# A convolution chain in fp32: group 0's first layer from raw row copies, and M products on quarters of ij

## The chip, the cores and the metric

The kernel runs on one core of one Trainium2 chip. The metric is the device time of one execution in microseconds, the median of several runs. The engines named below are TensorE (PE in the profile; its weight loads are PEld), VectorE (DVE), ScalarE (ACT), GpSimd (POOL) and SyncE (SP, which here only issues loads).

## The reference, cut to what matters

The input `x` is 4 x 32 x 32 x 16 (batch, row, column, channel). Three convolution layers and one interval layer are added to it, each on a group-normalized copy:

```python
def conv_ref(inputs, M, W, G):                 # layers 0, 1 and 3
    first = einsum('ijyx,byxc->bijc', M, inputs)          # the "M product"
    shifted = conv3x3(inputs, kernels from G)             # 32*32*16 filters of 3x3x16
    diff = relu(inputs - shifted)                         # (layer 3 the same, in another layout)
    second = einsum('ijyx,bijyxc->bijc', W, diff)
    return first - second

def _gn(v, G=8, eps=1e-5):                     # mean and variance over (h, w, 2 channels), per batch
    ...
x = x + conv_ref(_gn(x), L0...)
x = x + conv_ref(_gn(x), L1...)
x = x + interval_ref(_gn(x), L2...)            # pooling over intervals, small matmuls, sigmoids
x = x + conv_ref(_gn(x), L3...)
```

Every one of the 1024 positions (i, j) has its own 3x3 filter per feature. The convolution is computed as matmuls of filters with a matrix of shifted rows of the image (`im`), and the subtraction of `inputs` is folded into the filters (`pick`).

## The kernel before

The batches form two groups of two (`NG = 2`, `GB = 2`), so `GC = 32` columns of (batch, channel) per group. Layers and groups alternate in six phases. A phase runs over eight chunks of 128 positions (i, j), 16 features and 2 batches: 256 steps of six matmuls (in three slots) and one eviction.

```python
# one step (f, b) of conv_layer
ps = bank_pair(...)                            # 3 of these in PSUM
for slot in range(3):
    for h in range(2):                         # two halves of the image, on rows 0-63 and 64-127 of the array
        r = slice(64 * h, 64 * h + 64)
        w, v = (W9[r], im9v[r, b]) if slot == 2 else (W[r, slot], imv[r, slot, b])
        nc.tensor.matmul(ps[:, h, :], lhsT=w[:, f % FU, :], rhs=v[:, :, :H],
                         start=slot == 0, stop=slot == 2)
nc.vector.scalar_tensor_tensor(junk, ps, 0.0, chunks[n], op0=ALU.min, op1=ALU.mult,
                               accum_out=acc[...])
wait -= 1
if wait <= 0:
    wait = next(behind, 1 << 20)               # work of the next phase, spread between the steps
```

Eight features of filters come in one load (`raw`, four buffers). `prep` subtracts `pick` on GpSimd and scales slot 2 on ScalarE into `W9`; `prep_rest` (the halving step) finishes `W9` on VectorE. `W9` and `im9` are in fp32r, and carry the ninth tap.

Before a convolution the group is normalized, turned, written to DRAM and gathered back as shifted rows:

```python
def before_conv(g, layer, on_pe=False):
    xn = work.tile([P, NT, GC], F32, tag="xn", bufs=2)
    yield from group_norm(g, ..., xn, on_pe)   # sums, mean, xc, squares, rstd, xn
    nc.vector.transpose(xt[g][:, :, 1 : 1 + H], xn)
    for r in range(ROWS):
        (nc.scalar if r % 2 else nc.sync).dma_start(inner[:, r], xt[g][GC * r : GC * (r + 1)])   # xs <- xt
    for slot, row, tap in ...:                 # 12 of them, for 2 halves: 24 loads
        (nc.scalar, nc.sync)[at % 2].dma_start(
            im[g][r0 : r0 + C, slot, :, :RUN], xsv[:, :, off : off + RUN])                         # im <- xs
    halve(im9[g], im[g][:, 2], low_x)          # ScalarE
    halve_rest(im9[g], im[g][:, 2], low_x)     # VectorE
```

For five of the six phases this runs beside the phase ahead. For the first phase it stands alone at the start:

```python
nc.scalar.dma_start(X[0], x[0])
load_raw(0); load_chunk(0)                     # on SyncE's queue
...
start = before_conv(*phases[0], on_pe=True)    # sums across partitions by a matmul with ones
next(start)
# ... pick, low_w, low_x from the identity ...
for _ in start: pass
prep(0); prep_rest(0)
for phase in range(len(phases)):
    conv_layer(phase, behind(phase))
```

The M product of a layer and group, once per phase, in the stream of `behind`:

```python
def first_term(g, layer):
    fs = work.tile([P, 2, 512], F32, tag="fs")
    for half in range(2):                      # halves of ij
        mt = wpool.tile([P, NT, 512], F32, tag="MT", bufs=1)
        nc.sync.dma_start(mt, convs[layer][0][half])
        yield 12
        ps = bank(...)                         # pf
        for pt in range(NT):                   # eight parts of the sum over (y, x), on four column groups
            j = pt % 4
            nc.tensor.matmul(ps[32 * j : 32 * j + 32, :], lhsT=xn[:, pt, :], rhs=mt[:, pt, :],
                             start=pt < 4, stop=pt >= 4, tile_position=(0, 32 * j))
        nc.scalar.copy(fs[:, half, :], ps)
        yield 2
    ps = bank(...)                             # pfs
    for t in range(NT):                        # add the four partial sums and turn
        nc.tensor.matmul(ps[:, GC * t : GC * (t + 1)],
                         lhsT=fs[:, t // 4, t % 4 * P : (t % 4 + 1) * P], rhs=stack, start=True, stop=True)
    yield 2
    nc.vector.tensor_tensor(X[g], X[g], ps..., ALU.add)
```

The four column groups of the array (32 columns each, by `tile_position`) each hold a partial sum over a quarter of the terms; the matmuls with `stack` (four identities of 32 on top of each other) add them.

Of the kernel before, what the change touches and what calls it, by code (L numbers as in the profile page):

```python
# [14 lines left out]
P = 128  # L15
B, H, C = 4, 32, 16
NG = 2
# [20 lines left out]
def net_kernel(ctx: ExitStack, tc: tile.TileContext, x, convs, iv_w, iv_b, out):  # L38
# [30 lines left out]
    nc.scalar.dma_start(X[0], x[0])  # L69
# [16 lines left out]
    load_raw(0)  # L86
    load_chunk(0)


    ones = const.tile([P, P], F32, name="ones")  # L90
    nc.vector.memset(ones, 1.0)
# [29 lines left out]
    im = [const.tile([P, 3, GB, PITCH], F32, name=f"im{g}") for g in range(NG)]  # L121
    im9 = [const.tile([P, GB, PITCH], F32R, name=f"im9{g}") for g in range(NG)]

    def zeros(g):

        nc.gpsimd.memset(xt[g], 0.0)
        nc.gpsimd.memset(im[g][:, 2], 0.0)
        for y in (0, HP - 1):
            nc.gpsimd.dma_start(xs[g][:, y * HP : (y + 1) * HP], zero[:GC])

    nc.gpsimd.memset(zero, 0.0)
    zeros(0)

    def prep(u):

        if u >= n_chunks * NU:
            return
        raw = raws.pop(u)
        f0 = u % NU * FU
        nc.gpsimd.tensor_tensor(  # L140
            raw[:, 1], raw[:, 1],
            pick[:, f0 : f0 + FU].unsqueeze(2).to_broadcast([P, FU, P]),
            ALU.subtract,
        )
        W9 = wpool.tile([P, FU, P], F32R, tag="W9", name=f"W9_{u}")
        halve(W9, raw[:, 2], low_w)
        units[u] = (raw, W9)

    def prep_rest(u):
        if u in units:  # L150
            raw, W9 = units[u]
            halve_rest(W9, raw[:, 2], low_w)
# [9 lines left out]
    def group_norm(g, name, dst, on_pe=False):  # L162
# [9 lines left out]
        def mean_of(part, name):  # L172
            if not on_pe:
                m = work.tile([P, GC // 2], F32, tag="sum", name=f"sum_{name}")
                nc.gpsimd.partition_all_reduce(m, part, channels=P, reduce_op=bass_isa.ReduceOp.add)  # L175
                return m
            ps = bank(f"ps_{name}")
            nc.tensor.matmul(ps[:, : GC // 2], lhsT=ones, rhs=part, start=True, stop=True)  # L178
            return ps[:, : GC // 2]
# [25 lines left out]
    def before_conv(g, layer, on_pe=False):  # L205
        xn = work.tile([P, NT, GC], F32, tag="xn", bufs=2, name=f"xn_{g}_{layer}")
        xns[g] = xn
        yield from group_norm(g, f"c{g}{layer}", xn, on_pe)
# [27 lines left out]
    def first_term(g, layer):  # L236
# [3 lines left out]
        fs = work.tile([P, 2, 512], F32, tag="fs", name=f"fs_{g}{layer}")  # L240
        for half in range(2):
            mt = wpool.tile([P, NT, 512], F32, tag="MT", bufs=1, name=f"MT_{g}{layer}{half}")
            nc.sync.dma_start(mt, convs[layer][0][half])
            yield 12
            ps = bank(f"pf_{g}{layer}{half}")
# [339 lines left out]
```

## Time and profile before

| | |
|---|---|
| time, median of 3 runs | 3106.62 us (3105.61 to 3107.74) |
| span of the profiled execution | 3100.8 us |
| convolution matmuls, fp32 slots | 12288 entries of 64x512, mean 589 ns, overlapping |
| evictions (junk) | 1536, mean 1224 ns |
| M products (pf) | 192 entries, mean 598 ns; busy 23.1 us |
| adding the partial sums (pfs) | 96 entries, six blocks |
| HBM traffic | 211.64 MB read, 69 GB/s over the span |

The page gives the busy time of each engine, its course over 40 slices of the span, the chain of work that ended last (followed back from the last instruction), and the costliest groups of instructions by line, with output and inputs by their names in the program. In a row of the timeline the columns are start, length, engine, line, operation, tiles and shape, and in brackets the idle time of the engine just before and what ended it. An fp32 matmul shows as two entries. Names such as pc, pf and pfs are the PSUM tiles of the convolution, of the M product and of its summation; ps_l is a small matmul of the interval layer; xs and xt are the DRAM and SBUF forms of the turned input.

### The profile page before, as it was taken

Reading aid. Unit: us, or ns where it says so; the run is one execution under the profiler, and the core shown is the slowest. Engines: PE = TensorE matmul, PEld = TensorE weight load, DVE = VectorE, ACT = ScalarE, POOL = GpSimd, SP = SyncE. Lnnn points to the kernel's source line nnn. Section 1 sums busy time; section 2 is a strip of 40 time slices with the busy share of each in tenths; the row PEclk is TensorE's granted clock in tenths of the full one; section 3 lists DMA queues with packets and bytes.
Section 4 is the critical chain, followed back from the end, with each engine's and each line's share of the span. In section 5 each row is a group of like instructions: output and inputs, shape, how many; then the busy total and the mean of one; then the engine's idle time right before and its main releaser. Section 6 shows DMA issues by size and latency. Waiting matters only on the chain.

```text
span 3100.8 us, 37902 instructions
## 1 busy us (share of the span) xinstructions
PE 3069.8 (99%) x15760; PEld 1506.1 (49%) x15760; DVE 2114.4 (68%) x3361; ACT 145.7 (5%) x151; POOL 294.3 (9%) x182
## 2 busy tenths in 40 slices
PE   6999999999999999999999999999999999999999
PEld 3444444444444544444445444444544444454544
DVE  5666666766666666666678876668876666666666
ACT  0000000000000000000000000000000000000000
POOL 1100000100000000000012310001330000000000
PEclk9999999999999999999999999999999999999999
DMA  4331111421111141211111113121113211121100
GB/s 143 125 129 49 51 66 48 125 75 68 48 64 60 53 141 48 75 48 68 48 58 65 48 69 126 48 75 48 68 48 110 91 48 70 48 75 48 68 28 2
DMA packets 37068, 215.19 MB, mean 69 GB/s; under 512 B 11808, under 2 KB 12320, under 8 KB 23072
## 3 DMA queue, kind: packets, MB, share of 16 engines
q1 hardware_dynamic: 29472, 207.02, 18.6%
q10 hardware_dynamic: 7296, 5.74, 0.9%
q8 instruction: 123, 2.02, 0.3%
q14 instruction: 49, 0.40, 0.0%
q0 software_dynamic: 128, 0.02, 0.0%
HBM read 211.64 MB, written 1.12 MB: 69 GB/s over the span
## 4 chain that ended last, share of the span: by engine, by line
PE 99%; DMA 1%; DVE 0%; issue 0%; ACTq 0%; ACT 0%; DVEq 0%
PE pc L463 97%; PE pf L248 1%; PE pfs L256 0%; DMA im<-xs 0%; DMA X<-in_x 0%; DVE junk L473 0%; PE ps_r L376 0%; PE ps_l L365 0%; DMA xs<-xt 0%; PE ps_l L363 0%; DVE xc_c L188 0%; DVE pp L323 0%; PE ps_y L427 0%; PE ps_vc L178 0%; DVE xt L212 0%
## 5 line engine op out<-in xcount | busy, mean ns | idle before, releaser
L463 PE MATMUL pc<-im,raw 64*128 64x512 f32 x12288 | 2907.4, 589 | 15.3 <-DMA im<-xs 13.3
L473 DVE SCALAR_TENSOR_TENSOR junk<-pc,WT 128x1024 f32<-128x1024 f32 x1536 | 1879.7, 1224 | 958.5 <-PE pc L463 953.2
L463 PEld LDWEIGHTS pc<-im,raw 64*128 64x128 f32 x12288 | 1187.5, 186 | 1185.1 <-issue 800.5
L463 PE MATMUL pc<-im,W 64*128 64x512 f32 x3072 | 1251.1, 804 | 0.0
L463 PEld LDWEIGHTS pc<-im,W 64*128 64x128 f32 x3072 | 298.7, 186 | 365.8 <-issue 364.8
L140 POOL TENSOR_TENSOR raw<-raw,pick 128x1024 f32<-128x1024 f32 x96 | 182.5, 1902 | 1989.2 <-DMA raw<-in_g 1835.6
L111 ACT ACTIVATE W<-raw,low_w 128x1024 fp32r<-128x1024 f32 x96 | 110.4, 1150 | 2268.9 <-PE pc L463 2233.0
L114 DVE SCALAR_TENSOR_TENSOR W<-raw,low_w,W 128x1024 fp32r<-128x1024 f32 x96 | 134.6, 1402 | 0.0
L473 DVE DVE_READ_ACCUMULATOR junk<-pc,WT 128x1 f32 x1536 | 127.2, 83 | 0.0
L396 POOL TENSOR_TENSOR dp_a<-ft_a,rt_r 128x1089 f32<-128x1089 f32 x16 | 39.0, 2445 | 76.3 <-DVE s_a L403 49.5
L396 POOL TENSOR_TENSOR dp_b<-ft_b,rt_r 128x1089 f32<-128x1089 f32 x16 | 37.1, 2325 | 94.6 <-ACT ft_b L389 47.8
L248 PE MATMUL pf<-MT,xn 128*32 128x512 f32 x192 | 23.1, 598 | 0.0
L403 DVE TENSOR_REDUCE s_b<-dp_b 128x33 f32<-128x1089 f32 x16 | 20.5, 1282 | 0.0
L403 DVE TENSOR_REDUCE s_a<-dp_a 128x33 f32<-128x1089 f32 x16 | 20.5, 1282 | 0.0
L175 POOL PARTITION_ALL_REDUCE sum_mc<-part_mc x5 | 2.2, 445 | 188.3 <-DVE part_mc L167 188.3
L252 ACT COPY fs<-pf 128x512 f32<-128x512 f32 x12 | 7.0, 585 | 240.7 <-PE pf L248 240.7
L114 DVE SCALAR_TENSOR_TENSOR im<-im,low_x,im 128x1088 fp32r<-128x1088 f32 x6 | 8.1, 1347 | 13.3 <-DMA im<-xs 13.3
L485 DVE TENSOR_TENSOR X<-X,acc 128x32 f32<-128x32 f32 x48 | 11.8, 246 | 1.5
L256 PEld LDWEIGHTS pfs<-stack,fs 128*128 128x128 f32 x96 | 11.2, 191 | 3.4 <-issue 3.4
L338 DVE TENSOR_TENSOR pp<-pp 64x1024 f32<-64x1024 f32 x10 | 12.1, 1213 | 0.0
L343 DVE TENSOR_TENSOR pp<-pp 64x1024 f32<-64x1024 f32 x10 | 12.1, 1212 | 0.0
L175 POOL PARTITION_ALL_REDUCE sum_mi<-part_mi x2 | 0.9, 446 | 116.2 <-DVE part_mi L167 116.2
(77 smaller groups left out, 136.9 us busy)
## 6 DMA issues: line engine op xcount, KB each, us to landing
raw<-in_g SPq DMA_DIRECT2D x96, 1536.0 KB, 6.7
WT<-in_w SPq DMA_DIRECT2D x48, 512.0 KB, 6.5
MT<-in_mt SPq DMA_DIRECT2D x12, 2048.0 KB, 8.1
im<-xs SPq DMA_DIRECT2D x72, 67.8 KB, 3.0
im<-xs ACTq DMA_DIRECT2D x72, 67.8 KB, 3.0
xs<-xt SPq DMA_DIRECT2D x12, 34.0 KB, 2.8
xs<-xt ACTq DMA_DIRECT2D x12, 34.0 KB, 3.0
X<-in_x ACTq DMA_DIRECT2D x2, 128.0 KB, 7.3
```

The costliest lines, as they stand in the source:

```text
L111: nc.scalar.activation(dst, src, AF.Copy, scale=mask[:, 1:2])
L114: nc.vector.scalar_tensor_tensor(dst, src, mask[:, 0:1], dst.bitcast(F32), op0=ALU.mult, op1=ALU.add)
L140: nc.gpsimd.tensor_tensor(raw[:, 1], raw[:, 1], pick[:, f0 : f0 + FU].unsqueeze(2).to_broadcast([P, FU, P]), ALU.subtract,)
L248: nc.tensor.matmul(ps[32 * j : 32 * j + 32, :], lhsT=xn[:, pt, :], rhs=mt[:, pt, :], start=pt < 4, stop=pt >= 4, tile_position=(0, 32 * j),)
L256: nc.tensor.matmul(ps[:, GC * t : GC * (t + 1)], lhsT=fs[:, t // 4, t % 4 * P : (t % 4 + 1) * P], rhs=stack, start=True, stop=True,)
L338: nc.vector.tensor_tensor(pp[k][:, :H, M:], a[:, :H, M:], a[:, s : H + s, M:], ALU.max)
L343: nc.vector.tensor_tensor(pp[k][:, :H, M:], a[:, :H, M:], a[:, :H, M - s : M - s + H], ALU.max)
L396: nc.gpsimd.tensor_tensor(t, ft[:, i, :].unsqueeze(1).to_broadcast([P, T1, T1]), rt, ALU.add,)
L403: nc.vector.tensor_reduce(s[:, i - 1, :], last, axis=AX.X, op=ALU.max)
L463: nc.tensor.matmul(ps[:, h, :], lhsT=w[:, f % FU, :], rhs=v[:, :, :H], start=slot == 0, stop=slot == 2,)
L473: nc.vector.scalar_tensor_tensor(junk, ps.rearrange("p h n -> p (h n)"), 0.0, chunks[n], op0=ALU.min, op1=ALU.mult, accum_out=acc[:, t, co ...
L485: nc.vector.tensor_tensor(X[g][:, t], X[g][:, t], acc[:, t], ALU.add)
```

## The change

It has two parts.

**The start.** For the first phase (group 0, layer 0) the host gives the shifted rows of the raw input, `xi`, in the very layout of `im`, with zeros at the border, and a copy `xq` of the group's input with (quarter of the image, batch, channel) on the 128 partitions. The kernel loads both, takes mean and variance from `xq` with three small matmuls against masks, and normalizes `im` in place: subtract the mean, multiply by the reciprocal of the standard deviation, and set what lies outside the image to zero again. It works on batch 0 first, the filters of the first load are split in two parts (two features, then six), and the first 16 steps of the first chunk are sorted so that batch 0's eight features come before batch 1's. Batch 1 is normalized on GpSimd beside these steps, and the usual group norm of group 0, which the M product still needs, moves into the stream beside the convolution. What this is for: to start the convolution without the way through DRAM.

**The M product.** Each column group of the array now takes a quarter of ij instead of a part of the sum: all eight parts are added in PSUM, so no summation of partial sums is needed. VectorE turns the result by 32x32 blocks straight from PSUM, for which the host orders M's columns.

```diff
-    nc.scalar.dma_start(X[0], x[0])
+    XQ = const.tile([P, 256], F32, name="XQ")
+    nc.sync.dma_start(XQ, xq)
...
-    load_raw(0)
+    F0 = 2
+    raws[0] = wpool.tile([P, 3, FU, P], F32, tag="raw", bufs=4, name="raw_0")
+    nc.sync.dma_start(im[0][:, :, 0], xi[0])
+    nc.scalar.dma_start(raws[0][:, :, :F0], convs[0][2][0, 0][:, :, :F0])
     load_chunk(0)
+    nc.sync.dma_start(raws[0][:, :, F0:], convs[0][2][0, 0][:, :, F0:])
+    nc.sync.dma_start(im[0][:, :, 1], xi[1])
...
     def first_term(g, layer):
         xn = xns[g]
-        fs = work.tile([P, 2, 512], F32, tag="fs", name=f"fs_{g}{layer}")
+        ps = bank(f"pf_{g}{layer}")
         for half in range(2):
-            mt = wpool.tile([P, NT, 512], F32, tag="MT", bufs=1, name=f"MT_{g}{layer}{half}")
+            mt = wpool.tile([P, NT // 2, 4, 256], F32, tag="MT", bufs=1, name=f"MT_{g}{layer}{half}")
             nc.sync.dma_start(mt, convs[layer][0][half])
             yield 12
-            ps = bank(f"pf_{g}{layer}{half}")
-            for pt in range(NT):
-                j = pt % 4
-                nc.tensor.matmul(
-                    ps[32 * j : 32 * j + 32, :], lhsT=xn[:, pt, :], rhs=mt[:, pt, :],
-                    start=pt < 4, stop=pt >= 4, tile_position=(0, 32 * j),
-                )
-            nc.scalar.copy(fs[:, half, :], ps)
-            yield 2
-        ps = bank(f"pfs_{g}{layer}")
-        for t in range(NT):
-            nc.tensor.matmul(
-                ps[:, GC * t : GC * (t + 1)], lhsT=fs[:, t // 4, t % 4 * P : (t % 4 + 1) * P],
-                rhs=stack, start=True, stop=True,
-            )
+            for k in range(NT // 2):
+                pt = NT // 2 * half + k
+                for j in range(4):
+                    nc.tensor.matmul(
+                        ps[32 * j : 32 * j + 32, :256], lhsT=xn[:, pt, :], rhs=mt[:, k, j, :],
+                        start=pt == 0, stop=pt == NT - 1, tile_position=(0, 32 * j),
+                    )
         yield 2
+        ft = work.tile([P, NT * GC], F32, tag="fs", name=f"ft_{g}{layer}")
+        nc.vector.transpose(ft, ps[:, : NT * GC])
+        yield 1
         nc.vector.tensor_tensor(
-            X[g], X[g], ps[:, : NT * GC].rearrange("p (t m) -> p t m", t=NT), ALU.add
+            X[g], X[g], ft.rearrange("p (t m) -> p t m", t=NT), ALU.add
         )
...
+            steps = [(f, b) for f in range(C) for b in range(GB)]
+            if n == 0:
+                steps.sort(key=lambda s: (s[0] // FU, s[1]))
+            for at, (f, b) in enumerate(steps):
+                if at % (FU * GB) == 2:
+                    load_raw(u + 3)
+                if at % (FU * GB) == (8 if u == 0 else 2):
+                    prep(u + 1)
+                if at % (FU * GB) == (12 if u == 0 else 8):
+                    prep_rest(u + 1)
...
-    start = before_conv(*phases[0], on_pe=True)
-    next(start)
+    # pairs, own, to_rows, to_own, rows, kept: masks from the identity, on VectorE (cut)
+    def first_stats(src, name):
+        ps = bank(f"ps_{name}")
+        by_batch = work.tile([P, GB], F32, tag="by_batch", name=f"by_batch_{name}")
+        nc.vector.tensor_scalar_mul(by_batch, own, src)
+        nc.tensor.matmul(ps[:, :GB], lhsT=to_rows..., rhs=by_batch, start=True, stop=True)
+        return ps[:, :GB]
+
+    nc.vector.tensor_reduce(s1, XQ, axis=AX.X, op=ALU.add)
+    nc.tensor.matmul(ps[:, :1], lhsT=to_own..., rhs=s1, start=True, stop=True)
     # pick, low_w, low_x as before
+    nc.vector.tensor_copy(mean_own, ps[:, :1])
+    nc.vector.tensor_scalar_sub(XQ, XQ, mean_own)
+    nc.vector.scalar_tensor_tensor(squares, XQ, 1.0, XQ, op0=ALU.mult, op1=ALU.mult, accum_out=s2)
+    var = first_stats(s2, "v0")
+    m = first_stats(s1, "m0")
+    nc.vector.tensor_copy(mean0, m)
+    nc.vector.tensor_scalar_mul(minus_mean0, m, -1.0)
+    nc.scalar.activation(rstd0, var, AF.Sqrt, bias=eps)
+    nc.vector.reciprocal(rstd0, rstd0)
+    # normal(eng, b, slot): in place on im[0][:, slot, b]; sides(eng, b, slot): the border to zero (cut)
+    prep(0, 0, F0)
+    normal(nc.scalar, 0, 2)
+    for slot in range(2):
+        normal(nc.vector, 0, slot)
+        sides(nc.vector, 0, slot)
+    sides(nc.gpsimd, 0, 2)
+    prep_rest(0, 0, F0)
+    halve(im9[0][:, 0], im[0][:, 2, 0], low_x)
+    halve_rest(im9[0][:, 0], im[0][:, 2, 0], low_x)
+    prep(0, F0, FU)
+
+    def rest_of_start():                       # first in the stream of behind(0)
+        nc.sync.dma_start(X[0], x[0])
+        prep_rest(0, F0, FU)
+        for slot in (2, 0, 1):
+            normal(nc.gpsimd, 1, slot)
+            sides(nc.gpsimd, 1, slot)
+        yield 4
+        halve(im9[0][:, 1], im[0][:, 2, 1], low_x)
+        yield 1
+        halve_rest(im9[0][:, 1], im[0][:, 2, 1], low_x)
+        nc.gpsimd.memset(zero, 0.0)
+        zeros(0)
+        xns[0] = work.tile([P, NT, GC], F32, tag="xn", bufs=2, name="xn_00")
+        yield from group_norm(0, "c00", xns[0])
```

On the host, `xi`, `xq` and the new order of M's columns are laid out.

## Prediction

> **What bounds the kernel now.** I read the page first, then the chain of waits in order of time, then single stretches of the timeline.
>
> ```profile
> span 3100.8 us, 37902 instructions
> PE 3069.8 (99%) x15760; PEld 1506.1 (49%) x15760; DVE 2114.4 (68%) x3361; ACT 145.7 (5%) x151; POOL 294.3 (9%) x182
> ...
> PE pc L463 97%; PE pf L248 1%; PE pfs L256 0%; DMA im<-xs 0%; DMA X<-in_x 0%; DVE junk L473 0%; PE ps_r L376 0%; PE ps_l L365 0%; DMA xs<-xt 0%; PE ps_l L363 0%; DVE xc_c L188 0%; DVE pp L323 0%; PE ps_y L427 0%; PE ps_vc L178 0%; DVE xt L212 0%
> ```
>
> These are the span, the busy time and the chain by line. TensorE is on the chain for 97% with the convolution matmuls (pc), which the change does not touch. What can move is what stands before the first of them, what TensorE does between them (pf, pfs), and the tail. The chain by time has the start:
>
> ```profile
> 0.79 7.30 DMA X<-in_x
> ...
> 9.44 1.46 DVE xc_c L188
> ...
> 14.52 3.34 DMA xs<-xt
> 18.03 2.50 DMA im<-xs
> 20.61 2.78 DMA im<-xs
> 23.41 2.32 DMA im<-xs
> 25.78 2.28 PE pc L463 x4
> ...
> 28.23 3.93 PE pc L463 x13
> ```
>
> The columns are start, length (us) and what. The first convolution matmul starts at 25.78, after the load of X, the group norm, the way out to DRAM (xs) and three rounds of row gathers (im). And the M products of group 0, in the same view:
>
> ```profile
> 165.91 1.85 PE pf L248 x16
> 167.76 4.12 PE pc L463 x20
> 171.89 1.90 PE pfs L256 x16
> 173.79 29.63 PE pc L463 x150
> ```
>
> What such a block costs shows in the evictions (junk) on VectorE, in its timeline:
>
> ```profile
> 165.94 1.23 DVE L473 SCALAR_TENSOR_TENSOR junk<-pc,WT 128x1024 f32<-128x1024 f32 x1 [0.73 <-PE pc L463]
> 169.97 1.23 DVE L473 SCALAR_TENSOR_TENSOR junk<-pc,WT 128x1024 f32<-128x1024 f32 x1 [2.79 <-PE pc L463]
> 171.92 1.22 DVE L473 SCALAR_TENSOR_TENSOR junk<-pc,WT 128x1024 f32<-128x1024 f32 x1 [0.72 <-PE pc L463]
> 175.99 1.23 DVE L473 SCALAR_TENSOR_TENSOR junk<-pc,WT 128x1024 f32<-128x1024 f32 x1 [2.83 <-PE pc L463]
> ```
>
> Over the 1536 evictions the usual distance is 1.964 us. Across the pf block it is 169.97 - 165.94 = 4.03, so 2.06 more; across pfs 175.99 - 171.92 = 4.07, 2.11 more. Over all blocks I measure 2.05 for a pf half and 2.10 for a pfs block. The whole span is then: first eviction at 30.49, plus 1535 x 1.964 = 3014.7, plus 50.8 of longer distances, plus 4.5 from the last eviction's start to the end: 3100.5 of 3100.8. Of the 50.8, 12 pf halves make 24.6, 6 pfs blocks 12.6, and the interval layers with one VectorE wait near 1610 the other 13.6. All the work of VectorE, ScalarE, GpSimd and the loads in the steady part is hidden.
>
> **What the Trainium skill says.** (1) TensorE: Matmul & The Clock Gate, section The mechanism: matmuls on different tiles of the array overlap, and a weight load for another tile is pulled ahead of matmuls in flight. The trace agrees: in a pf block four matmuls on four groups of 32 columns start 7 ns apart, the next four 0.43 us later, with the 110 ns weight loads in between hidden. (2) Same page, section What's actually happening: the array runs at half clock until about 3.4 us of sustained work. Agrees: the first passes of 512 columns after 25.78 are 0.985 us apart, and from about 29.5 they are 0.43. (3) SBUF — State Buffer, section Who interferes with whom: a VectorE instruction with two SBUF inputs contends with a GpSimd instruction that reads SBUF. Agrees: the halving step of W9 takes 1.28 us, but 4.27 at 1609.14 while GpSimd works from 1609.19 on; xc takes 1.45 in the start, beside GpSimd's subtraction, for work that takes 0.43 elsewhere (sq). (4) VectorE: DVE Perf Modes, section The perf-mode tier table: tensor_scalar on fp32 in SBUF can run at 2x. No row before shows it; the in-place normalization will.
>
> **The change, part by part: the start.** Nothing goes through DRAM any more; the host's copy of the shifted rows comes in one transfer per batch. I follow the chain, with durations from rows of the same size before.
> - XQ is the first load. Before, the first packets of the first queue start at 1.82 and take 1.0 to 1.8 us, and X's last packet ended 7.38 and had landed at 8.09, so 0.7 for completion. XQ is 8 packets of 1 KB on each of 16 engines at 46 ns, taken in turns with those of ScalarE's queue: done about 3.4, landed about 4.1. VectorE's fifteen small constants from 1.6 on (0.07 to 0.25 us each by the rows pick, low_w, low_x) end about then too.
> - s1 sum of 256 elements 0.42: 4.5. Small matmul and copy: 0.70 from VectorE to VectorE (8.53 to 9.23 before): 5.2 plus 0.2. Subtract 0.35, squares 0.5: 6.3. by_batch 0.15, matmul 0.6, by_batch again (it waits for that matmul, as its buffer is single) 0.15, matmul 0.6: 8.0. Two copies and the reciprocal 0.5: 8.5. The square root on ScalarE lies beside this.
> - Batch 0's rows: 24 packets of 2176 B at about 88 ns per engine (between 46 for 1 KB and 159 for 4 KB) behind XQ, mixed with the first two filters: landed about 7.1, not the last wait.
> - Normalize slot 0: 542 elements, 0.45 (an estimate between 2x of note 4 and the plain rate of the 1.28 for 1024), three narrow edge multiplies 0.4: 9.35. TensorE starts about 9.4, not 25.78.
> - Slot 1 on VectorE ends about 10.2, its two halving steps about 11.3 (256 elements 0.35, 544 elements 0.7; ScalarE's three 0.65 us steps and GpSimd's two memsets end about 10.5). TensorE at half clock needs 2 x 0.985 per slot: slot 0 until 11.4, slot 1 until 13.2, slot 2 until 13.4. So once it starts, the clock sets the first chunk, and VectorE has 1.5 to 2 us of slack.
> - First eviction about 13.6 instead of 30.49: **-16.9 us**. The rest of the filters (landed about 11.3, subtraction until 12.8, needed about 16), batch 1's rows (landed about 13.4, GpSimd until about 18.5, needed at 13.4 + 7 x 1.96 = 27) and the second group norm (beside the convolution; each all-reduce keeps GpSimd about 7.5 us, as the idle 7.22 after 51.81 before) have room. This is why batch 0's eight features go first.
>
> **The M products.** 16 matmuls of 512 columns per layer become 32 of 256 in two halves, the same columns streamed (the trace shows every fp32 matmul as two passes, so a half is 16 entries now and 32 after). Each column group now keeps a quarter of ij, so no partial sums have to be added, and the eight pfs matmuls go. A half is now eight rounds of four matmuls at 213 ns instead of four at 427. Rounds this short exist already: ps_l, 264 columns on four groups.
>
> ```profile
> 1744.85 0.58 PE ps_l L363 x8
> 1745.42 0.58 PE ps_l L365 x8
> ```
>
> There two rounds take 0.58 us; their starts are 0.24 apart, the rest is drain and refill. So the weight loads (102 to 110 ns) fit inside a 213 ns round, and a half stays at 8 x 0.215 + 0.14 = 1.86: 12 x 0.02 = **+0.2 us**. The pfs blocks go: 6 x 2.10 = **-12.6 us**. The transpose of 128x256 on VectorE (0.45 by the row of xt) and the loss of ScalarE's copies (12 x 0.585) are off the chain, as VectorE idles 0.73 us in each 1.964.
>
> **Sum.** 3106.6 - 16.9 - 12.6 + 0.2 = 3077.3; I add 0.7 for a likely wait in the first chunks (below): **3078 us**, 0.9% faster.
>
> **Rivals.**
> 1. VectorE and GpSimd collide in the first chunks. The halving of the remaining six filters (768 elements) stands behind the first eviction, at about 14.9, just when GpSimd normalizes batch 1 with few gaps; TensorE needs it at about 17. For it: the 4.27 at 1609. Against: GpSimd's memsets and waits between its steps leave gaps. Cost 0 to 3 us: up to 3081.
> 2. The weight loads no longer hide: 32 loads of 110 ns one after the other would be 3.5 us a half, +1.7 x 12 = 20 us, and the time would be 3097. Against: in ps_l eight pairs take 0.58, not 0.9 and more. I give it 4%. A milder form, 0.24 per round, adds 0.2 x 12 = 2.4.
> 3. The loads are the start's bound: the first filters, the rows and XQ share the engines, and X before took 7.3 us for 128 KB beside a larger load. If XQ landed at 7 instead of 4.1, the gain falls by 3: 3081.
> 4. The one wait near 1610 comes from who is first by 50 ns, GpSimd or VectorE:
>
> ```profile
> 1609.14 4.27 DVE L114 SCALAR_TENSOR_TENSOR W<-raw,low_w,W 128x1024 fp32r<-128x1024 f32 x1
> 1609.19 1.27 POOL L329 TENSOR_SCALAR_AFFINE_SELECT pp<-pp 64x1024 f32<-64x1024 f32 x1 [14.80 <-ACT pp L327]
> ```
>
> It costs TensorE 2.0; at the same place of group 1 (2127) VectorE won and nothing was lost. It can vanish (3076) or come twice (3080).
>
> **Range and chances.** The start is good to about 2.5 us, the M products to 2.4, the collisions to 2 each way with a longer tail upward. 3073 to 3084 holds it 8 times in 10. Over 2% faster would be below 3044, 34 us more than all parts together can give: 1%. Over 2% slower needs a loss that no part suggests: 1%. Within 2%: 98%.
>
> **What would show it.** In the changed profile: first pc matmul at 9 to 10, first eviction at 13 to 14.5, no gathers (im from xs) before it; no pfs in the chain, pf blocks of 1.85 to 1.95 with 32 matmuls; the eviction distance still 1.964. Wrong would be pf blocks over 2.2 us, an idle TensorE between 14 and 45, or a longer usual distance.

## The result, and the profile after

| | before | after |
|---|---|---|
| time, median of 6 runs | 3105.78 us (3104.74 to 3107.74) | 3080.19 us (3077.04 to 3081.59) |
| ratio | | 0.9915, 95% interval 0.9902 to 0.9928 |
| span of the profiled execution | 3100.8 us | 3075.7 us |
| first eviction | 30.49 us | 14.02 us |
| first to last eviction | 3065.83 us | 3057.22 us |
| last eviction to the end | 4.47 us | 4.47 us |

The predicted time was 3078 us, a gain of 28.6; the measured gain is 25.6 (25.1 between the two profiled spans). The last three lines of the table add up to each span, so the gain has two parts: 16.47 at the start and 8.61 in the steady part, and nothing at the end. Of the six runs after, two took 3077.0 and 3077.4 us and four 3079.6 to 3081.6; the profile is of the run of 3077.43, so the account below is of that one, and what the four spent more is not shown.

The page of the changed kernel, its span, busy times and chain by line:

```profile
span 3075.7 us, 38109 instructions
PE 3059.3 (99%) x15858; PEld 1989.4 (65%) x15858; DVE 2125.9 (69%) x3397; ACT 141.1 (5%) x144; POOL 301.5 (10%) x197
...
PE pc L460 98%; PE pf L251 1%; DVE junk L470 0%; DMA im<-in_xi 0%; PE ps_r L370 0%; PE ps_l L359 0%; DVE pp L317 0%; PE ps_l L357 0%; PE ps_y L421 0%; DVE im L592 0%; DVE im L600 0%; SPq L73 0%; DVE X L482 0%; DVE W L125 0%; DVEq L600 0%
```

The gathers (im from xs) and the summation (pfs) have left the chain, as intended. One number nobody asked for stands out: the weight loads (PEld) are busy for 1989.4 us instead of 1506.1, with only 98 more of them. The chain in order of time, at the start and around the first M products:

```profile
1.23 7.50 DMA im<-in_xi
...
8.84 0.58 DVE im L600
...
9.44 0.40 DVE im L592 x2
...
10.16 19.94 PE pc L460 x91
```

```profile
166.91 1.86 PE pf L251 x32
168.78 23.75 PE pc L460 x114
```

Columns are start, length and what. The start is now a load of batch 0's rows that lands at 8.73, the normalization, the edges, and TensorE at 10.16. A pf block with 32 entries takes 1.86 us, and the convolution follows at once. Later the same chain shows something that was there once before and is now there twice, a stretch in which TensorE waits for an eviction that stands behind the halving step of W9. VectorE and GpSimd in the timeline of the changed kernel:

```profile
1585.38 4.27 DVE L125 SCALAR_TENSOR_TENSOR W<-raw,low_w,W 128x1024 fp32r<-128x1024 f32 x1
1585.42 1.27 POOL L323 TENSOR_SCALAR_AFFINE_SELECT pp<-pp 64x1024 f32<-64x1024 f32 x1 [15.04 <-ACT pp L321]
...
1586.68 1.89 POOL L149 TENSOR_TENSOR raw<-raw,pick 128x1024 f32<-128x1024 f32 x1
...
1589.57 1.21 DVE L470 SCALAR_TENSOR_TENSOR junk<-pc,WT 128x1024 f32<-128x1024 f32 x1
```

```profile
2101.64 4.27 DVE L125 SCALAR_TENSOR_TENSOR W<-raw,low_w,W 128x1024 fp32r<-128x1024 f32 x1
2105.83 1.21 DVE L470 SCALAR_TENSOR_TENSOR junk<-pc,WT 128x1024 f32<-128x1024 f32 x1
```

The halving step takes 4.27 us instead of 1.28, the eviction behind it is late, and PSUM runs out. TensorE then stands idle for 1.77 us until the eviction is done:

```profile
1590.85 0.70 PE L460 MATMUL pc<-im,raw 64*128 64x512 f32 x2 [1.77 <-DVE junk L470]
```

This happens in the interval layers of both groups, at 1585 and at 2102.

**A measure used below.** The array takes each convolution matmul in two halves, rows 0-63 and rows 64-127, each with its own weights. From the trace I take the starts of the slot-2 matmuls on each half; the second's start minus the first's, step by step, is the lag between the halves. In the kernel before it stays within 30 ns in 99% of the 1536 steps (mostly 3 to 10 ns; the rest are in the interval layers). In the changed kernel the two halves start together until the first pf block at 166.9; from there they leave each other: one takes 1963.3 ns per step and the other 1960.0 (in the kernel before both take 1961.7), until the lag stays at -453 ns. The pf blocks bring them together again, and after each they part anew; in the last phase the lag grows the other way, to 1094 ns at the end. It is over 30 ns in 80% of the steps. When the halves are apart, their weight loads no longer lie side by side, which is why PEld's busy time rose. That was a second suspect for lost time. (The expectations of experiments 9 and 10 speak of lags of 1.5 to 2 us; there a start was held against the step before, so that -0.45 us read as 1.51.)

### The profile page after: what moved, and what is told of

Its sections match the earlier page's. It is cut to its first block, busy times and chain, and to the rows that moved or that the text cites. A ratio compares the mean times of both kernels' runs of the same rounds, so it can differ in the third digit from the quotient of the medians.

```text
span 3075.7 us, 38109 instructions
## 1 busy us (share of the span) xinstructions
PE 3059.3 (99%) x15858; PEld 1989.4 (65%) x15858; DVE 2125.9 (69%) x3397; ACT 141.1 (5%) x144; POOL 301.5 (10%) x197
## 3 DMA queue, kind: packets, MB, share of 16 engines
q8 instruction: 124, 2.03, 0.3%
## 4 chain that ended last, share of the span: by engine, by line
PE 99%; DVE 0%; issue 0%; DMA 0%; SPq 0%; DVEq 0%
PE pc L460 98%; PE pf L251 1%; DVE junk L470 0%; DMA im<-in_xi 0%; PE ps_r L370 0%; PE ps_l L359 0%; DVE pp L317 0%; PE ps_l L357 0%; PE ps_y L421 0%; DVE im L592 0%; DVE im L600 0%; SPq L73 0%; DVE X L482 0%; DVE W L125 0%; DVEq L600 0%
## 5 line engine op out<-in xcount | busy, mean ns | idle before, releaser
L460 PE MATMUL pc<-im,raw 64*128 64x512 f32 x12288 | 2996.0, 589 | 5.8 <-DVE junk L470 3.5
L460 PEld LDWEIGHTS pc<-im,raw 64*128 64x128 f32 x12288 | 1664.8, 186 | 723.5 <-issue 443.5
L460 PE MATMUL pc<-im,W 64*128 64x512 f32 x3072 | 1645.3, 805 | 0.0
L460 PEld LDWEIGHTS pc<-im,W 64*128 64x128 f32 x3072 | 478.5, 186 | 328.8 <-issue 276.3
L149 POOL TENSOR_TENSOR raw<-raw,pick 128x1024 f32<-128x1024 f32 (+1 forms) x97 | 182.2, 1879 | 1921.0 <-DMA raw<-in_g 1854.5
L122 ACT ACTIVATE W<-raw,low_w 128x1024 fp32r<-128x1024 f32 (+1 forms) x97 | 110.7, 1141 | 2458.4 <-PE pc L460 2457.0
L125 DVE SCALAR_TENSOR_TENSOR W<-raw,low_w,W 128x1024 fp32r<-128x1024 f32 (+1 forms) x97 | 138.2, 1425 | 0.0
L251 PE MATMUL pf<-MT,xn 128*32 128x256 f32 x384 | 23.2, 382 | 0.0
L251 PEld LDWEIGHTS pf<-MT,xn 128*32 128x32 f32 x384 | 11.2, 109 | 13.1 <-issue 6.9
L122 ACT ACTIVATE im<-im,low_x 128x1088 fp32r<-128x1088 f32 (+1 forms) x7 | 7.5, 1073 | 114.0 <-DMA im<-xs 109.6
```

The lines of the kernel that those rows point to most:

```text
L122: nc.scalar.activation(dst, src, AF.Copy, scale=mask[:, 1:2])
L125: nc.vector.scalar_tensor_tensor(dst, src, mask[:, 0:1], dst.bitcast(F32), op0=ALU.mult, op1=ALU.add)
L149: nc.gpsimd.tensor_tensor(raw[:, 1, at:to], raw[:, 1, at:to], pick[:, f0 + at : f0 + to].unsqueeze(2).to_broadcast([P, to - at, P]), ALU.s ...
L251: nc.tensor.matmul(ps[32 * j : 32 * j + 32, :256], lhsT=xn[:, pt, :], rhs=mt[:, k, j, :], start=pt == 0, stop=pt == NT - 1, tile_position= ...
```

## The experiments

The parts of the change are first taken apart (1, 2), then the long waits (3), the array's clock (4), the lag of the halves (5, 6, 9, 10) and the load of the rows (11). All times stand beside runs of the kernel before on the same chip in the same sitting; these gave 3103.59 us for experiments 1 to 4, 3104.86 for 5 to 8, and 3105.1 for 9 to 11.

| experiment | median us | ratio, 95% interval | span us | first eviction | first to last eviction |
|---|---|---|---|---|---|
| 1 start alone | 3089.43 | 0.9953 (0.9940 to 0.9965) | 3087.9 | 14.42 | 3068.99 |
| 2 M product alone | 3091.63 | 0.9960 (0.9947 to 0.9974) | 3090.6 | 32.26 | 3053.88 |
| 3 halving earlier | 3073.12 | 0.9901 (0.9888 to 0.9915) | 3071.1 | 13.64 | 3053.02 |
| 4 warm array | 3077.77 | 0.9917 (0.9903 to 0.9930) | 3076.8 | 13.44 | 3058.86 |
| 5 as 3, filters moved by 64 B | 3072.32 | 0.9896 (0.9882 to 0.9909) | 3071.0 | 14.72 | 3051.82 |
| 6 before, filters moved by 64 B | 3108.75 | 1.0012 (1.0006 to 1.0019) | 3105.7 | 31.71 | 3069.50 |
| 7 3, 5 and warming | 3071.64 | 0.9895 (0.9880 to 0.9910) | 3069.5 | 13.63 | 3051.41 |
| 8 the changed kernel again | 3077.37 (one run) | | 3075.6 | 13.95 | 3057.21 |
| 9 as 3, filters moved by 128 B | 3072.81 (one run) | | 3071.1 | 13.69 | 3052.94 |
| 10 as 3, rows and filters moved by 64 B | 3073.03 (one run) | | 3071.3 | 13.74 | 3053.11 |
| 11 as 5, rows loaded ahead of the filters | 3071.27 | 0.9893 (0.9876 to 0.9909) | 3069.6 | 13.52 | 3051.58 |

### 1. The new start with the old M product

```diff
 # the changed kernel, with first_term of the kernel before
-            for k in range(NT // 2):
-                ...  # 32 matmuls of 256 columns, a quarter of ij per column group
+            for pt in range(NT):
+                ...  # 16 of 512 columns, a part of the sum per column group
+            nc.scalar.copy(fs[:, half, :], ps)
+        # and the eight pfs matmuls with stack
```

> The new start with the M product of before (pf in halves of 512 columns, then pfs). Theory A (the two parts add up, and the start is worth 16.5 us of the span, as the first evictions 30.49 and 14.02 say): span 3100.8 - 16.5 = 3084.3, or 3086.3 if the second collision of GpSimd and VectorE near 2100 belongs to the start's shift of the data; six pfs blocks of 1.9 us are in the chain again. Theory B (the 3 us that the whole change fell short come from the start, as its work runs on beside the convolution): span 3087 or more, with longer eviction distances in the first 100 us. On the two halves of the array: if they run out of step here as well (one 1963.3 ns per step, the other 1960.0, where before both took 1961.7), the cause lies in the start or in where its tiles stand in SBUF; if they keep step, in the new M product.

Measured: first eviction at 14.42, so 16.1 us earlier, but the steady part is 3.16 us longer than before (3068.99 against 3065.83). It splits into 1.02 in the first step, because the array's clock stayed at half for some 6.1 us here (the changed kernel: some 3.3), nothing from the waits (one of 2.0 us at 2114 in place of the one of 2.0 at 1612), and 2.1 from the halves of the array, which are out of step as in the changed kernel. So the start brings its 16 us, and what is given back later comes with the start and not with the M product.

### 2. The new M product with the old start

```diff
 # the kernel before, with first_term of the changed kernel and M in its order
+            for k in range(NT // 2):
+                pt = NT // 2 * half + k
+                for j in range(4):
+                    nc.tensor.matmul(ps[32 * j : 32 * j + 32, :256], lhsT=xn[:, pt, :], rhs=mt[:, k, j, :],
+                                     start=pt == 0, stop=pt == NT - 1, tile_position=(0, 32 * j))
+        nc.vector.transpose(ft, ps[:, : NT * GC])
```

> The kernel before with the new M product alone (quarters of ij, turned by VectorE). Theory A: 6 x 2.10 for the pfs blocks less 12 x 0.01 for slightly longer halves: span 3100.8 - 12.5 = 3088.3, with pf blocks of 1.86 us. Theory B (the new pf blocks leave the two halves of the array out of step, which costs about 2 us): span near 3090.3, and the two halves drift from the first pf block on. If they keep step, the drift of the whole change comes from the start or from the places of the tiles.

The steady part shrinks from 3065.83 to 3053.88, by 11.95. Take off what is chance in it: the first step was 0.47 longer here (the gathers ended later, and the clock was still at half), and one wait at the interval layer of 2.02 against 2.03. Then 3063.79 becomes 3051.39, a gain of **12.40**; the prediction's terms for the M product are 12.6 - 0.2 = 12.4. The halves keep step here: a lag of 117 ns, there since the first steps, stands still until the first pf block and is about 10 ns from there on. The first eviction came 1.8 us later than in the profiled execution of before, in a start that this kernel has not changed.

### 3. The halving step three steps earlier

```diff
-                if at % (FU * GB) == (12 if u == 0 else 8):
+                if at % (FU * GB) == (12 if u == 0 else 5):
                     prep_rest(u + 1)
```

> The changed kernel with the halving step of W9 on VectorE at step 5 of 16 instead of step 8, so that it is over when GpSimd begins its affine select in the two interval layers. Theory A (that collision is what costs 2.0 us at each of 1588 and 2104): both long distances go, span 3075.7 - 4.1 = 3071.6. Theory B (the four transposes of VectorE just before are what makes it late, the halving only shows it): at most 1 us is won. Theory C (another pair collides in its place): nothing won, with long distances elsewhere.

Both long waits are gone, and with them 4.20 us of the steady part (3057.22 to 3053.02): step by step, 2.0 at each of the two waits and 0.3 near 2150, behind the second. VectorE at the same place of the interval layer:

```profile
1578.19 1.28 DVE L125 SCALAR_TENSOR_TENSOR W<-raw,low_w,W 128x1024 fp32r<-128x1024 f32 x1
1579.39 1.22 DVE L470 SCALAR_TENSOR_TENSOR junk<-pc,WT 128x1024 f32<-128x1024 f32 x1
...
1585.26 1.23 DVE L470 SCALAR_TENSOR_TENSOR junk<-pc,WT 128x1024 f32<-128x1024 f32 x1
```

and GpSimd there:

```profile
1585.11 1.27 POOL L323 TENSOR_SCALAR_AFFINE_SELECT pp<-pp 64x1024 f32<-64x1024 f32 x1 [16.39 <-ACT pp L321]
1586.37 1.89 POOL L149 TENSOR_TENSOR raw<-raw,pick 128x1024 f32<-128x1024 f32 x1
```

The halving step now runs 7 us ahead of GpSimd's two instructions and takes 1.28 us; the evictions, which read one operand from PSUM, stay at 1.22 to 1.23 beside the same GpSimd work. The halves are out of step as before (PEld 1992.7 us), so that is a separate matter.

### 4. Keeping the array awake ahead of the first pass

```diff
+    def warm(name, times):                    # results are never read
+        ps = bank(f"warm_{name}")
+        for k in range(times):
+            nc.tensor.matmul(ps[:, :P], lhsT=ident, rhs=ident, start=True, stop=True)
     ...                                       # after the first small matmul of the statistics
+    warm("a", 4)
     ...                                       # after the last one
+    warm("b", 5)
```

> The changed kernel with nine matmuls of ident with itself on TensorE between and behind the statistics' matmuls, whose result nobody reads, so that the array has worked for some microseconds when the first convolution matmul comes. Theory A (the half clock sets the first chunk): passes of 0.43 instead of 0.85 to 0.98 us from the start; VectorE's halving, which ends at 12.4, is then the last wait, and the first eviction comes at about 12.9 instead of 14.02: span about 1.1 us less. Theory B (VectorE's chain sets the first chunk): first eviction where it was, within 0.2. Theory C (so little work does not raise the clock): passes as slow as before.

```profile
8.10 2.50 PE L547 MATMUL warm_b<-ident 128*128 128x128 f32 x10 [0.32 <-DVE minus_mean L584]
...
10.54 2.61 PE L460 MATMUL pc<-im,raw 64*128 64x512 f32 x8
```

The rows are the timeline of TensorE in this kernel. The first passes are 1.01 and 0.57 us apart, and then 0.43: so the full clock came at about 11.8, 3.7 us after the second burst of warming began. That is near what the Trainium skill has (TensorE: Matmul & The Clock Gate, section What's actually happening: about 3.4 us of sustained work, in windows that run freely, so that the moment varies). But the warming itself held the array until 10.54, although the edges were done at 9.42, so the first eviction gained 0.58 us and not the whole of the slow passes. The steady part took 3058.86 here, 1.64 more than in the changed kernel, all of it within 20 us behind the second wait, which with that cost 3.7 us instead of 2.0. This ate the gain; what made it longer is not shown.

The variation is real: in the kernels with the new start the passes went from 0.85 to 0.43 us some 3.3 us after the first one in the changed kernel, 4.0 in its second execution, 4.3 in experiment 3, 4.6 in 11, 5.1 in 5 and 6.1 in 1, with nearly the same instructions ahead of it. (The moment is worked out from the length of the pass in which the clock rose.)

### 5 and 6. Moving the filters by 64 bytes

The kernel before has the rows (im) at a multiple of 128 B in each partition of SBUF, and the filters (raw, W9) 64 B past one. The change allots its constants otherwise, and there both lie at a multiple of 128 B. (The places follow from the order and the sizes in which kernel.py allots its tiles.) A spare tile of 64 B undoes that in experiment 5 (on top of 3) and does it in experiment 6 (on the kernel before). It moves all that is allotted behind it by as much, the chunks of W (WT) and M's tiles (MT) too.

```diff
+    pad = const.tile([P, 16], F32, name="pad")     # 64 B per partition; 6 has it behind im9
+    nc.vector.memset(pad, 0.0)
     eps = const.tile([P, 1], F32, name="eps")
```

> The changed kernel with the early halving step, and a tile of 64 B per partition put before the filters, so that raw and W9 start 64 B off a multiple of 128 B, as in the kernel before (in the changed kernel and in the start-only kernel they start at a multiple of 128 B; in the kernel before and in the M-product-only kernel they do not). Theory A (where the filters stand decides whether the two halves of the array keep step): both halves take 1961.7 ns per step, the lag between them stays under 20 ns, and the span falls by about 2 us from 3071.1 to 3069. Theory B (the drift comes from the state in which the new start leaves the array): lag and span as in the early-halving run.

> The kernel before with the same 64 B put between the image rows and the filters, so that raw and W9 start at a multiple of 128 B. Nothing else is changed. Theory A: the two halves now drift apart here, one at 1963.3 and one at 1960.0 ns per step, and the span grows by about 2 us from 3100.8 to 3103. Theory B: they keep step, span 3100.8 within the 1.7 us by which the start of the kernel differs from run to run.

The lag of the halves answers. In experiment 5 it is about 10 ns, and over 30 in only 0.8% of the steps, as in the kernel before, and the page shows the weight loads side by side again:

```profile
PE 3057.8 (100%) x15858; PEld 1520.1 (49%) x15858; DVE 2118.3 (69%) x3398; ACT 141.1 (5%) x144; POOL 300.4 (10%) x197
```

In experiment 6 the kernel before, whose only other difference is a memset, goes out of step, and already ahead of the first pf block: the lag is 139 ns at its second step and grows to 312 at the block. Later it runs from -453 to +799 ns:

```profile
PE 3073.9 (99%) x15760; PEld 1978.5 (64%) x15760; DVE 2115.8 (68%) x3362; ACT 145.7 (5%) x151; POOL 295.5 (10%) x182
```

In time experiment 5 fell short of what was expected. Its first eviction came at 14.72, 1.1 later than in 3, since its rows landed at 9.05 instead of 7.45, with the same loads; the steady part is 1.20 shorter, and 1.6 when what the first step took over the usual distance (0.49 and 0.10) is taken off. Experiment 6 lost 3.67 in the steady part: its wait at the interval layer, which stood at the second group this time, cost 3.7 us as in experiment 4, where before it cost 2.0; that leaves 2.0 for the halves.

### 7. Everything together

Experiment 3, the spare tile of 5, and 4, 4 and 3 warming matmuls ahead of, between and behind the small matmuls of the statistics.

> The early halving, the 64 B, and matmuls of ident with itself in three places of the start (four before the statistics, four and three between and behind them), shorter behind them than in the first such run, where they kept TensorE until 10.5. If the clock is up when the first convolution matmul comes at about 9.4 to 10.2, slot 0 and slot 1 take 0.86 each and VectorE's halving (about 11.8 to 12.4) is the last wait: first eviction 12.4 to 13.0, span 1 to 1.5 us under the run with early halving and 64 B, so about 3067.5. If the clock is not up, the first eviction is at 13.4 or later and nothing is won.

3071.64 us; first eviction 13.63, steady part 3051.41, halves in step. The clock rose some 2.9 us after the first matmul, and the first eviction came 3.66 us after it, where 4.25 were needed in experiment 5. So warming gained 0.6; but the rows landed only at 8.55 and the first matmul came at 9.97. It is no faster than experiment 11, which warms nothing.

### 8. The changed kernel once more

> The changed kernel once more, unaltered, for one look at its start. If the time at which the array's clock rises is a matter of chance, the first convolution matmul should come at 9.4 to 10.2 as before, but the first eviction can differ from 14.02 by more than 0.5 us, as in the start-only run, whose clock rose about 2 us later; the two waits near 1588 and 2104 should be there again. If both agree within 0.2 us, the differences of the other runs come from their edits.

3057.21 from first to last eviction, against 3057.22 the first time: the two waits recur, and so do the lags from the first pf block on (-239, -449, -20, -233, -439 and -452 ns at steps where the first execution had -239, -448, -19, -232, -439 and -453). They are no chance of one execution, but belong to this kernel. Its first eviction came at 13.95, within 0.07 us of the first time, but that hides two differences that cancel: the rows landed at 8.30 instead of 8.74, and the clock rose 4.0 instead of 3.3 us after the first matmul. So this kernel repeats itself in the steady part, and at the start it does not.

### 9 and 10. Is it the spare tile, the filters, or rows against filters?

```diff
 # 9
+    pad = const.tile([P, 32], F32, name="pad")     # 128 B
 # 10: the 64 B tile stands ahead of im, so that im, raw and W9 are all 64 B past a multiple of 128
+    pad = const.tile([P, 16], F32, name="pad")
     im = [const.tile([P, 3, GB, PITCH], F32, name=f"im{g}") for g in range(NG)]
```

> The run with the halving at step 5, with a spare tile of 128 B instead of 64 per partition, so that the filters start at a multiple of 128 B as in the changed kernel. Theory A (where the filters lie against 128 B decides whether the halves of the array keep step): out of step again from the first pf block on, lags of about 1.5 to 2 us between the halves as in the changed kernel, first to last eviction 3053.0 us. Theory B (any spare tile, or the one more instruction at the start, did it): in step, lag about 10 ns, 3051.8.

> As the run with the spare 64 B, but the spare tile stands ahead of the rows im too, so that rows and filters both start at 64 B past a multiple of 128. Theory A1 (rows and filters must differ in that place): out of step, lags of 1.5 to 2 us, first to last eviction about 3053. Theory A2 (the place of the filters alone counts): in step, lag about 10 ns, 3051.8.

Both are out of step: PEld 2014.5 and 1995.4 us, lags from -453 to +840 and to +1093 ns, steady parts 3052.94 and 3053.11. In 9 the course of the lag differs from that of 3 (it grows to +840 ns where 3 stays at -452, and ends at -453 where 3 ends at +1093); in 10 it is that of 3, nearly everywhere within 2 ns. So a spare tile as such does nothing, and the place of the filters alone does not decide it: of the places tried, the halves keep step where rows and filters lie 64 B apart within 128 B, and lose it where they lie alike. Which of the tiles that move with the filters matters, and why, no run here shows.

### 11. The rows ahead of the filters

```diff
     nc.sync.dma_start(im[0][:, :, 0], xi[0])
-    nc.scalar.dma_start(raws[0][:, :, :F0], convs[0][2][0, 0][:, :, :F0])
+    nc.sync.dma_start(raws[0][:, :, :F0], convs[0][2][0, 0][:, :, :F0])
     load_chunk(0)
```

> As the run with the spare 64 B, but the first two filters are loaded on SyncE's queue behind batch 0's rows instead of on ScalarE's queue beside them. Theory A (the rows landed at 8.8 instead of 7.1 us because they shared the transfer engines with the filters): rows landed by about 7.5, the normalization waits for the statistics instead and starts at 8.2 to 8.3, first convolution matmul at 9.5 to 9.7. Theory B (the rows take that long by themselves): landed at 8.5 to 9 as before, and the filters land later, up to 1 us on the start. Time between 3071.0 and 3072.5.

The rows no longer share the transfer engines with the filters, and the normalization waits for the statistics. From the timeline of this kernel:

```profile
5.16 0.43 DVE L571 SCALAR_TENSOR_TENSOR squares<-XQ 128x256 f32<-128x256 f32 x1
...
7.61 0.61 POOL L151 TENSOR_TENSOR raw<-raw,pick 128x256 f32<-128x256 f32 x1 [6.03 <-DMA raw<-in_g]
7.79 0.74 DVE L602 TENSOR_SCALAR im<-im,mean,rstd 128x542 f32<-128x542 f32 x1
...
9.28 3.78 PE L462 MATMUL pc<-im,raw 64*128 64x512 f32 x8 [1.86 <-DVE im L594]
```

and the same instructions of the changed kernel:

```profile
5.16 0.61 POOL L149 TENSOR_TENSOR raw<-raw,pick 128x256 f32<-128x256 f32 x1 [3.58 <-DVE XQ L566]
5.17 0.88 DVE L569 SCALAR_TENSOR_TENSOR squares<-XQ 128x256 f32<-128x256 f32 x1
...
8.84 0.56 DVE L600 TENSOR_SCALAR im<-im,mean,rstd 128x542 f32<-128x542 f32 x1 [0.63 <-DMA im<-in_xi]
...
10.16 3.58 PE L460 MATMUL pc<-im,raw 64*128 64x512 f32 x8 [2.29 <-DVE im L592]
```

In brackets stands the idle time and what ended it. The rows landed at 6.42 instead of 8.74, and the normalization starts as soon as the statistics are there, which is theory A. The filters then arrive later too, so GpSimd's subtraction moves away from the squares of the statistics (0.43 instead of 0.88) and falls on the normalization instead (0.74 instead of 0.56): the statistics end at 7.75 instead of 8.20. The first matmul is 0.88 earlier than in the changed kernel and 1.19 earlier than in experiment 5.

How much of that is due to the order of the loads, these runs do not show. In the nine executions with the loads of the changed kernel the rows landed at 7.40 (9), 7.45 (3), 7.67 (4), 7.74 (10), 8.30 (8), 8.55 (7), 8.74 (the changed kernel), 8.75 (1) and 9.05 us (5). In the first four of these they were not the last wait, as predicted. In experiment 3 the normalization follows the statistics at once, so no idle time stands in brackets:

```profile
8.07 0.56 DVE L600 TENSOR_SCALAR im<-im,mean,rstd 128x542 f32<-128x542 f32 x1
```

The first matmul came at 9.39 there, hardly later than the 9.28 of experiment 11. The rows of experiment 11 landed 1.0 us ahead of the earliest of the nine, so the filters beside them do cost time; but it is one execution, and where the 1.65 us between equal loads come from is not shown. At 3071.27 us this is the fastest median of the study, level with experiment 7; its ratio is 0.9893.

## Why the prediction was right, and where it was off

The time fell well inside the range. The sum shows what held, from the profiled spans; the working of the right-hand column is below.

| term of the sum | predicted | measured |
|---|---|---|
| start, to the first eviction | -16.9 | -16.5 |
| M products: pfs gone, pf blocks | -12.6 + 0.2 | -12.4 |
| wait in the first chunks | +0.7 | 0 |
| interval layers: one wait more | 0 (rival 4: -2 to +2) | +2.0 |
| halves of the array out of step | not foreseen | +1.8 |
| sum | -28.6 | -25.1 (the spans: -25.1) |

The last two come from a comparison with experiment 2, which has the same M products, one wait, and the halves in step. Eviction by eviction, the changed kernel falls behind it by 3.81 us from first to last (3057.22 against 3053.88, and 0.47 for experiment 2's slow first step). Of this, **2.0** are lost at the additional wait near 2102 and the other **1.8** evenly along the convolution steps. An eviction needs both halves, and so keeps the pace of the slower one: over the last steps (1360 to 1520) the mean distance of the evictions is 1963.33 ns in each of the eight executions that are out of step, and 1961.66 or 1961.67 in each of the five that are in step. In the interval layers nothing of this kind is lost. Other pairs give 1.4 to 1.6 us for the halves (3, 9 and 10 against 5, 7 and 11), 2.0 (6 against the kernel before) and 2.1 (1 against the kernel before).

Point by point:

- **The loads.** XQ landed at 2.86, where 4.1 was predicted, but its sum began only at 3.49, when VectorE was done with its constants. "Batch 0's rows ... landed about 7.1, not the last wait" is the step that failed in the profiled execution: they landed at 8.74 and were the last wait, by 0.63 us, on top of statistics that ended at 8.20 instead of 8.5 (the steps listed for them add up to 7.8, not 8.0, by the second small matmul). The queue was reckoned by its own packets, and the two filters on the other queue were given too little of the shared engines: with nothing of theirs beside them, the rows landed at 6.42 (experiment 11). How much of the 1.6 us is that, and how much the scatter of 7.40 to 9.05 between equal loads, stays open; in four executions the step held. This is rival 3 in a mild form, on another transfer than the one it named.
- **The normalization.** 0.56 instead of 0.45 for 542 elements, and 0.66 instead of 0.4 for three edge multiplies. By the plain rate (1.28 us for 1024 elements) 542 would take 0.68, by twice that 0.34. The 0.56 lies between, and part of it is a fixed cost, as the edge multiplies show; so the double rate of the fourth note is neither confirmed nor excluded.
- **The first eviction.** First matmul at 10.16 instead of 9.4, first eviction at 14.02 instead of 13.6. Of the 0.76 us lost, 0.34 came back by luck: the clock rose 3.3 us after the first matmul, before slot 2 was done. In the seven executions in which it rose later (1, 3, 5, 8, 9, 10 and 11) the first eviction came 4.23 to 4.25 us after the first matmul, where 4.2 had been predicted; in the changed kernel 3.86, and with warming 3.66 (7) and 2.90 (4). So "the clock sets the first chunk" held, and what scattered the first evictions from 13.44 to 14.72 was for the most part when the first matmul came (9.28 to 10.54).
- **The first chunks.** The 0.7 us for a likely wait was not needed. The halving step of six filters took 1.43 us at 15.17 beside GpSimd's normalization of 2.24, and TensorE did not wait. Rival 1 fell.
- **The M products.** Right to the tenth, blocks of 1.86 with 32 entries. The round of four loads and four matmuls takes 0.216 us. Rival 2 fell. (What the first note takes from its page is said there of loads for another group of rows or for the background weight buffer; the column groups of M share all rows, and that their loads are hidden is what the trace shows.)
- **Rival 4** was the right mechanism at twice the count, and the central value had left it at nought. Its wording, that it goes by "who is first by 50 ns", is not what the starts show: in all fourteen such meetings (the kernel before, both executions of the changed one, experiments 1, 2, 4 and 6) VectorE's halving started 42 to 47 ns ahead of GpSimd's instruction. VectorE took 1.28 us (and GpSimd 2.37 for its first instruction) in four and 4.27 in ten. Three of the four had the largest leads (46, 47 and 47 ns), but the fourth had 43, as had four of those that lost. Here is the one that it won in the kernel before, VectorE's row and then GpSimd's:

```profile
2127.26 1.28 DVE L114 SCALAR_TENSOR_TENSOR W<-raw,low_w,W 128x1024 fp32r<-128x1024 f32 x1
```

```profile
2127.31 2.37 POOL L329 TENSOR_SCALAR_AFFINE_SELECT pp<-pp 64x1024 f32<-64x1024 f32 x1 [14.89 <-ACT pp L327]
```

  Before, the lost meeting at 1609 looked much the same, 45 ns apart, but there VectorE took 4.27 us and GpSimd 1.27. The Trainium skill (SBUF — State Buffer, section Who interferes with whom) has it that the order of issue decides which of the two blocks. That one of them blocks the traces confirm; the order of their starts in the trace does not tell which. The remedy does not depend on that: three steps earlier, they do not meet.
- **The usual distance** between evictions (the median) stayed at 1.963 us in both kernels, so this sign was given as predicted. It was too coarse: the mean over steps 1360 to 1520 rose from 1961.66 to 1963.33 ns, as half of the array had slowed down while the other had become faster by as much, and the evictions follow the slower. The prediction holds nothing on the place of tiles in SBUF, so it could not see these 1.8 us.

The gain came out 3.0 us smaller than predicted (25.6 against 28.6; 25.1 between the spans). What the prediction had wrong is more than that: 2.0 for the wait, 1.8 for the halves and 0.4 at the start. The 0.7 that it had added for a wait that did not come hid a part of it, which is luck.

## What to carry to other kernels

When an engine off the critical path gets a long instruction with two SBUF operands next to work of GpSimd, move it some steps away rather than hope for the order: here three steps were worth 4.2 us, a sixth of the whole change. A change at the start of a kernel moves what stands in memory and what meets later, so after it compare the whole steady part (first to last of some regular instruction) and not only the stretch that was edited. And a transfer on the critical path is to be sized with everything on all queues that is in flight with it, and with the scatter of its landing (here 1.65 us between nine executions with equal loads).

## What the runs showed that had not been expected

- **Two halves of the array can run out of step for the rest of a kernel.** With rows and filters at the same place within 128 B of SBUF (0 and 0, or 64 and 64), the halves part, in seven executions at the first pf block and in experiment 6 at its second step, and differ by up to 1.09 us. The place alone does not start it: until the first pf block the lag of the changed kernel stood at 3 to 4 ns. With rows and filters 64 B apart (0 and 64) a lag, where there was one (117 ns in experiment 2, 84 in 7), stood still until the first pf block and was some 10 ns after it. It is seen at a glance in PEld's busy time, 1953 to 2015 us against 1506 to 1551. It costs 1.7 ns on every convolution step, 1.4 to 2.1 us of 3050. What in the array or the memory makes this was not found, and only these places were tried.
- **The time at half clock** was 3.3 to 6.1 us from the first pass in kernels with nearly the same start and no warming. Where it ended late it did not delay the first eviction further, but lengthened the step after it (by 1.02 us in experiment 1).
- **The same load landed at 7.40 to 9.05 us** in nine executions, which is most of the scatter of about 1 us in the first evictions.
- **GpSimd blocked VectorE through two instructions in a row** (1.27 and 1.89 us), though VectorE's had started 43 ns before the first of them.
- **A narrow VectorE instruction costs far more than its elements:** three multiplies of 16 elements per partition took 0.66 us, 0.2 each.
